# Moving the layer-0 xs stores to ScalarE's transfer queue, and the rank store half a unit later in SyncE's

## The chip, the cores and the metric

One Trainium2 chip, one of its cores. A core has TensorE (PE), VectorE (DVE), ScalarE (ACT), GpSimd (POOL) and SyncE (SP), each with a list of instructions of its own that it works through in order, and 16 DMA engines, which move data between the chip's main memory and the on-chip memory. A transfer is an instruction in the list of some engine: that engine issues it, and goes on while the data moves. Instructions wait for one another by semaphores. The metric is the time of one execution on the device in microseconds (us), less being better.

## The reference

The input x has 4 images of 64 channels and 256x256 points, in float32. Two layers follow one another; only the first is touched by the change.

```python
def layer0(x):                      # called with gn(x), a group norm in 32 groups
    h = gelu(conv3x3(x, c1_w) + c1_b)
    h = c1x1(h, c2_w, c2_b)
    xa, k = split(h, 2, axis=1)
    xs = depthwise_1x3(xa) + sh_b
    xs = depthwise_3x1(xs) + sv_b
    xs = gelu(xs)
    pooled = xs.mean(axis=(2, 3))
    weights = softmax(pooled @ gate_w.T)
    mask = top 2 of the 3 weights, per image, the rest 0
    out = xs
    for i, (w1, b1, w2, b2, w3, b3) in enumerate(experts):   # ranks 2, 4, 8
        e = c1x1(c1x1(k, w2, b2) * c1x1(xs, w1, b1), w3, b3)
        out = out + e * mask[:, i]
    return c1x1(out, proj_w, proj_b)

x = x + layer0(gn(x))
x = x + layer1(gn(x))   # two 3x3 convolutions with 8-bit weights and batch norms over all images
```

What matters for the change: the expert weights of an image depend on the mean of xs over the whole image. So the output of layer 0 can't be formed where xs is made. xs, and the product of the two low-rank maps, are kept in main memory until the image's gate is known, and are read back then.

## The kernel before, in words

*Units.* The front (layer 0) is cut into 64 units: 4 images of NCH = 16 chunks, each of 16 rows of the image. A loop over slots, u = 0 to SLOTS−1 with SLOTS = 67, puts the work of several units side by side: in slot u the convolution of unit u is done, the input for u+1 and u+2 is prepared, the depthwise taps of u−1 and u−2 are finished, and the output of a unit about an image back is formed. The layer's second convolution stage (conv1, conv2 of layer 1) follows it, and the last slots of the front overlap with conv1's first steps.

*Order.* Nothing is left to a scheduler in the main part: all five engines keep the order in which the program's calls are made. That order comes from a table of places. `at_slot(u, pos, call, ...)` puts a call at a place: a pos under 6 is in the first half of slot u, a pos from 6 on in its second half (pos 6.13 comes at order 0.13 there). Calls are then made in the order of their places, and each call appends its instructions to the lists of the engines that it uses. For the slots behind the last unit, a dictionary TAIL (L1023) says at which step of conv1 each call comes.

*Transfers.* All transfers of the loop are issued from SP (`nc.sync.dma_start`). SP's list has, per unit: the load of x (x_load, L508, 1.25 MB, three units ahead); a load of the input of the next image for its statistics (stats_load, L409, 1 MB, tile xs_in); the store of y, layer 0's output (out_store, L861, 1 MB, to y_d); the load of the input into the y tile, to which the layer's result is added (out_load, L803, 1 MB, tile y, of which there are 2); the load of xs back (xs_load, L812, 1 MB); two stores of xs (xs_store, L710, 512 KB each, to xs_d). In every second unit there are two loads of the experts' ranks (low_load, L822, 256 KB each) and one store of the ranks (in front_low, L747, 512 KB, to low_d). Eight completion semaphores are dealt out to the transfers in the order of the program, so a transfer also waits until the one eight before it, which used the same semaphore, has landed.

*Around xs.* Each unit makes two xs tiles, sub 0 and sub 1. For each: front_taps_a and front_taps_b (PE, tile ps_a, one buffer), front_taps_i (ACT, L677: t from ps_a), front_taps_h (DVE, L683, L686, L689: neighbours added in t), front_xs (ACT, L705: xs = gelu(t), its sum kept for the mean), xs_store. An xs tile has 4 buffers. In slot u, sub 1 of unit u−2 has its taps from 2 to 5.2, its gelu at 5.3 and its store at 8.6. Sub 0 of unit u−1 has its taps from 7 on, its gelu in the next slot at 1.55 and its store there at 4.7. Next to them on ACT stand x_four (L526, at 1.58) and the two gelus of front_h (L637, at 6.13 and 6.14).

*Around the ranks.* Over two units, front_k (PE) and front_k_out (ACT, L733, in even slots, at 9.2) form k·w2 in the tile k (1 buffer); front_q (PE, at 8 in odd slots) forms xs·w1; front_low (at 8.1 in odd slots) multiplies them on DVE (L746) and stores the result.

*Around y.* out_open (PE, tile ps_o) projects xs and the ranks with the gate's weights in them, out_add (DVE, L848) adds this to the y tile, out_stats (DVE, L853) takes the statistics of y, and out_store sends it to y_d. The table has out_store at 8.25, between the store of the ranks (8.1) and that of xs sub 1 (8.6).

Of the kernel before, what the change touches and what calls it, by code (L numbers as in the profile page):

```python
# [28 lines left out]
NOCT = NG // 2  # L29
# [12 lines left out]
def conv_preact_kernel(ctx: ExitStack, tc: tile.TileContext, io, col128, colset, col64):  # L42
    nc = tc.nc
# [18 lines left out]
    xs_d = [dram.tile([P, NOCT, 2 * GF], F32, name=f"xs_d{b}") for b in range(B)]  # L62
    low_d = [dram.tile([P, NOCT // 4, 2 * GF], F32, name=f"low_d{b}") for b in range(B)]
# [4 lines left out]
    def flat(t):  # L68
        return t.rearrange("p a b -> p (a b)")
# [50 lines left out]
    def at(step, order, call, *args):  # L120
        plan[step, order].append((call, args))
# [9 lines left out]
    def c128(name):  # L131
        return m128[:, col128[name][0] : col128[name][1]]
# [103 lines left out]
    def weights1_scale():  # L236
        tops = work.tile([P, P, 2], F32, tag="k", name="tops", bufs=1)
        rows = bass.AP(top_d.tensor, top_d.offset, [[0, P], [1, 2 * P]])
        nc.sync.dma_start(tops.rearrange("p a b -> p (a b)"), rows)
        yield  # L240
        for i, name in enumerate(("w1", "w2")):
            nc.vector.tensor_reduce(w_scale[name], tops[:, :, i], AX.X, ALU.max)

    def weights1(name):

        scale = w_scale[name]
        w = mset[0][:, colset[name][0] : colset[name][1]]
        nc.vector.tensor_scalar(scale, scale, 1.0 / QMAX, None, ALU.mult)
        inv = stat.tile([P, 1], F32, tag="s3", name=f"inv_{name}")
        nc.vector.reciprocal(inv, scale)  # L250
        yield
        nc.vector.tensor_scalar(w, w, inv, ROUND, ALU.mult, ALU.add)
        nc.vector.tensor_scalar(w, w, ROUND, None, ALU.subtract)
        nc.vector.tensor_scalar(w, w, QMAX, -QMAX, ALU.min, ALU.max)
        yield
        g = w.rearrange("p (k o) -> p k o", k=3)
        first, second = g[:, :, 0:P], g[:, :, P : 2 * P]
        nc.vector.tensor_copy(wq[name][:, 0], first)
        nc.vector.tensor_tensor(wq[name][:, 1], first, second, ALU.add)
        nc.vector.tensor_scalar(wq[name][:, 2], second, -1.0, None, ALU.mult)  # L260
# [216 lines left out]
    xt, x4s, e2s, mcs, d2s, hs, xss, k_sb, pooled, open_a, open_t = ({} for _ in range(11))  # L477
# [229 lines left out]
    def xs_store(u, sub):  # L707
        b, k = divmod(u, NCH)
        n = 2 * k + sub
        nc.sync.dma_start(xs_d[b][:, n, :], flat(xss[b, n]))  # L710

    def front_k(b, j):

# [29 lines left out]
    def front_low(b, j):  # L743
        ps = ps_q.pop((b, j))
        low = flat(k_sb.pop((b, j)))
        nc.vector.scalar_tensor_tensor(low, ps.rearrange("p s f -> p (s f)"), c128("e_b1"), low, ALU.add, ALU.mult)  # L746
        nc.sync.dma_start(low_d[b][:, j, :], low)  # L747

    ps_q, xs_in, open_o = {}, {}, {}
    wm, out_bias, ys, lows, st_y = {}, {}, {}, {}, {}  # L750
# [263 lines left out]
    def at_each(places, chain):  # L1014

        for place in places:
            at(*place, next, chain, None)
# [3 lines left out]
    SLOTS = UNITS + 3  # L1021

    TAIL = {  # L1023
        (0, 1.15): (0, 1.15), (0, 1.55): (0, 1.55), (0, 4.7): (0, 4.7), (0, 2): (0, 2), (0, 2.2): (0, 2.2),
        (0, 4): (0, 13.2), (0, 4.15): (0, 13.3), (0, 5.2): (0, 13.4), (0, 5.3): (0, 13.5), (0, 8.6): (1, 13.9),
        (0, 9.2): (3, 13.35), (0, 7): (2, 13.2), (0, 7.2): (2, 13.25), (0, 8): (3, 13.1), (0, 9): (3, 13.2), (0, 9.1): (3, 13.3),
        (1, 1.15): (3, 13.4), (1, 1.55): (3, 13.5), (1, 4.7): (4, 13.9), (1, 2): (5, 13.2), (1, 2.2): (5, 13.25),
        (1, 4): (6, 13.2), (1, 4.15): (6, 13.3), (1, 5.2): (6, 13.4), (1, 5.3): (6, 13.5), (1, 8.6): (7, 13.9),
        (1, 8): (8, 13.2), (1, 8.1): (8, 13.3),
    }  # L1030

    def at_slot(u, pos, call, *args):

        step, order = (2 * u, pos) if pos < 6 else (2 * u + 1, pos - 6)
        if u >= UNITS:
            step, order = TAIL[u - UNITS, pos]
            step += CONV1
        at(step, order, call, *args)

    def plan_front():  # L1040
        last = UNITS - 1
        at_slot(0, 0, x_load, 2)
        at_slot(0, 1.25, next, first_end, None)
        at_slot(0, 1.36, next, first_end, None)
        for u in range(SLOTS):
            if u + 3 <= last:
                at_slot(u, 0, x_load, u + 3)
            if u <= last:
                at_slot(u, 1, front_conv, u, (1, 2))
                at_slot(u, 1.1, front_copy, u, 0)  # L1050
                at_slot(u, 1.3, front_conv, u, (3, 4))
                at_slot(u, 1.35, butterfly_a, u)
                at_slot(u, 1.4, front_copy, u, 1)
                at_slot(u, 2.1, butterfly_b, u)
                at_slot(u, 4.05, butterfly_c, u)
                at_slot(u, 6.12, butterfly_d, u)
                at_slot(u, 6.13, front_h, u, True)
                at_slot(u, 5, front_conv, u, (0, 5))
                at_slot(u, 6.14, front_h, u, False)
            if u + 1 <= last:  # L1060
                if u == 0:
                    at_slot(u, 0.5, x_differences, 1)
                at_slot(u, 1.2, x_scaled, u + 1)
                at_slot(u, 1.31, v_inner, u + 1, 0)
                at_slot(u, 2.3, v_inner, u + 1, 1)
                at_slot(u, 5.5, v_outer, u + 1)
            if u + 2 <= last:
                at_slot(u, 1.58, x_four, u + 2)
                at_slot(u, 2.4, x_fourths, u + 2)
                at_slot(u, 6.6, x_seconds, u + 2, (0, 2))  # L1070
                at_slot(u, 7.3, x_seconds, u + 2, (4, 6))
            if 0 <= u - 2 <= last:
                at_slot(u, 2, front_taps_a, u - 2, 1)
                at_slot(u, 2.2, divide)
                at_slot(u, 4, front_taps_b, u - 2, 1)
                at_slot(u, 4.15, front_taps_i, u - 2, 1)
                at_slot(u, 5.2, front_taps_h, u - 2, 1)
                at_slot(u, 5.3, front_xs, u - 2, 1)
                at_slot(u, 8.6, xs_store, u - 2, 1)
            if 0 <= u - 1 <= last:  # L1080
                at_slot(u, 7, front_taps_a, u - 1, 0)
                at_slot(u, 7.2, divide)
                at_slot(u, 9, front_taps_b, u - 1, 0)
                at_slot(u, 9.1, front_taps_i, u - 1, 0)
                at_slot(u + 1, 1.15, front_taps_h, u - 1, 0)
                at_slot(u + 1, 1.55, front_xs, u - 1, 0)
                at_slot(u + 1, 4.7, xs_store, u - 1, 0)
            j = (u - 2) // 2
            if u % 2 == 0 and 0 <= j < UNITS // 2:
                at_slot(u, 8, front_k, *divmod(j, NOCT // 4))  # L1090
                at_slot(u, 9.2, front_k_out, *divmod(j, NOCT // 4))
            if u % 2 and 0 <= j < UNITS // 2:
                at_slot(u, 8, front_q, *divmod(j, NOCT // 4))
                at_slot(u, 8.1, front_low, *divmod(j, NOCT // 4))
        for b in range(B):
            t = NCH * (b + 1)
            if b < B - 1:
                places = (t + 1, 8.3), (t + 2, 1.25), (t + 2, 1.36), (t + 2, 1.52), (t + 2, 6.15), (t + 2, 8.3), (t + 2, 9.06)
                chain = gate(b)
                for place in places:  # L1100
                    at_slot(*place, next, chain, None)
            else:
                at_each(((CONV1 + 12 + n, 12.7) for n in (1, 3, 3, 4, 8, 12, 16)), gate(b))

        at_slot(1, 1.6, weights1_load)
        at_slot(3, 6.2, weights1_top)
        chain = weights1_scale()
        at_slot(4, 1.45, next, chain, None)
        at_slot(4, 6.2, next, chain, None)
        for i, name in enumerate(("w1", "w2")):  # L1110
            chain = weights1(name)
            for n in range(3):
                at_slot(7 + 3 * i + n, 6.2, next, chain, None)
# [67 lines left out]
    def plan_conv1(b):  # L1181
# [31 lines left out]
        at(t + NG + 3, 13.3, conv1_close, b)  # L1213

    plan_front()
    for b in range(B):
        if b < B - 1:
# [125 lines left out]
    with tc.manual_schedule(  # L1343
# [8 lines left out]
        n = len(chunks)  # L1352
# [62 lines left out]
    for i, (b, k) in enumerate(steps):  # L1415
# [9 lines left out]
        j = i - 3 + KEEP  # L1425
# [113 lines left out]
```

## Time and profile before

| | us |
|---|---|
| runs before | 3035.65, 3042.23, 3040.98 (median 3040.98) |
| the profiled execution | 3027.39 |
| its span in the trace | 3025.4 |
| front, units of layer 0 (changed) | about 0 to 1350 |
| conv1 and conv2 of layer 1 | about 1360 to 2600 |
| last stage, sums and output | about 2600 to 3025 |
| issue of one xs store on SP: least, median, most | 0.319, 0.383, 2.752 |

The page has the share of each engine over the whole span, then 40 slices of 75.6 us: a digit is a tenth of the slice in which the engine was busy, for DMA the mean over the 16 DMA engines. A list of waits gives, for an instruction's line, what it waited for, with the sum in us, the number of times and the longest one. SPq is the queue of SP, which has only transfers to issue. A row of windows gives, from left to right, the length of the stretch, the busy time of PE, PE's weight loads (PEld), DVE, ACT and POOL with their counts, PE's clock, the share of the transfers' time and what was moved in GB/s. A row of the timeline has start, duration, engine, line, operation and output <- input; a bracket at its end tells how long the engine idled before it, and what ended that. In all of these a wait for several things is put down to the one that came last.

The last 425 us are bound by transfers (425 GB/s, in the page's last slices), and the two convolution stages by PE in their larger part. None of them holds an instruction of the change, except for the last few xs stores and the last rank store, which TAIL puts into conv1's first steps.

### The profile page before, as it was taken

How to read it: one execution, taken by the hardware profiler on the slowest of the kernel's cores; microseconds unless marked ns; L12 is line 12 of the kernel's file. 1: busy time of each engine (PE TensorE's matmuls, PEld its weight loads, DVE VectorE, ACT ScalarE, POOL GpSimd, SP SyncE). 2: the span in 40 equal slices, each digit the busy share in tenths (PEclk: the TensorE clock that was granted, in tenths of full speed). 3: DMA queues.
4: the chain of work that ended last, by engine and by line, in shares of the span. 5: the costliest groups of instructions: out<-in, count | busy, mean ns of one | idle time of the engine just before them, and what ended most of it. 6: DMA issues, size and time to landing. Idle time of an engine off the chain costs nothing.

```text
span 3025.4 us, 53036 instructions
## 1 busy us (share of the span) xinstructions
PE 2364.3 (78%) x21576; PEld 1504.4 (50%) x21576; DVE 2467.0 (82%) x2793; ACT 2054.0 (68%) x2274; POOL 1677.4 (55%) x1210
## 2 busy tenths in 40 slices
PE   1898899998999999978889999989999999100000
PEld 1444444444544445545556667767888888100000
DVE  5668688888888899968788888979998998876665
ACT  6798887786876555556566677878888888432222
POOL 5888887776877778834445455635555555000000
PEclk9999999999999999999999999999999999655555
DMA  8565479999999879849889898756777763899999
GB/s 344 188 238 224 185 263 371 350 349 346 342 341 329 301 280 328 291 157 322 315 327 332 336 339 321 262 207 238 257 273 262 266 243 138 333 425 424 424 425 410
DMA packets 135572, 915.35 MB, mean 303 GB/s; under 512 B 14944, under 2 KB 15712, under 8 KB 40608
## 3 DMA queue, kind: packets, MB, share of 16 engines
q1 hardware_dynamic: 135328, 911.97, 80.3%
q8 instruction: 169, 2.77, 0.4%
q14 instruction: 75, 0.61, 0.1%
HBM read 573.74 MB, written 338.17 MB: 301 GB/s over the span
## 4 chain that ended last, share of the span: by engine, by line
PE 28%; DMA 18%; DVE 5%; issue 2%; ACT 1%; SPq 1%; POOL 0%; DVEq 0%; ACTq 0%
PE ps_h L295 18%; PE ps_h2m L295 6%; DMA y_end<-y_d 5%; DMA h<-h_d 4%; DMA out<-h 4%; PE ps_hm L295 3%; DMA y<-in_xp 3%; DMA xs_in<-xs_d 2%; PE ps_o L492 2%; DVE h L317 1%; DVE diff L352 1%; DVE y L848 1%; DVE odd L361 1%; DMA y_d<-y 1%; SPq L822 0%
## 5 line engine op out<-in xcount | busy, mean ns | idle before, releaser
L295 PE MATMUL ps_h<-diff,w_q 128*128 128x512 f32 x3072 | 751.3, 399 | 9.1 <-DVE h L317 9.1
L295 PEld LDWEIGHTS ps_h<-diff,w_q 128*128 128x128 f32 x3072 | 577.1, 189 | 180.9 <-issue 25.8
L492 PE MATMUL ps_c<-v,us 64*64 64x256 f32 x9216 | 547.2, 386 | 41.4 <-DVE ps_c L623 35.6
L342 POOL TENSOR_TENSOR d<-yn 128x1024 f32<-128x1024 f32 x128 | 355.0, 2793 | 313.7 <-DMA yn<-y_d 179.8
L492 PEld LDWEIGHTS ps_c<-v,us 64*64 64x64 f32 x9216 | 363.6, 136 | 199.8 <-DVE ps_c L623 44.9
L342 POOL TENSOR_TENSOR d<-h 128x1024 f32<-128x1024 f32 x127 | 311.9, 2477 | 194.8 <-DVE diff L350 130.0
L492 PE MATMUL ps_a<-h,av 64*64 64x512 f32 x4080 | 387.9, 493 | 38.8 <-DVE t L686 28.7
L317 DVE SCALAR_TENSOR_TENSOR h<-ps_h,scale_w,m 128x1024 f32<-128x1024 f32 x256 | 323.6, 1279 | 64.2 <-PE ps_h L295 48.1
L540 POOL TENSOR_TENSOR x<-x 128x512 f32<-128x512 f32 x256 | 330.3, 1290 | 12.5
L1420 ACT ACTIVATE v<-y_end,shift,gn 128x2048 f32<-128x2048 f32 x64 | 133.8, 2093 | 279.7 <-DMA y_end<-y_d 244.5
L492 PEld LDWEIGHTS ps_a<-h,av 64*64 64x64 f32 x4080 | 153.9, 134 | 307.5 <-issue 204.3
L381 ACT ACTIVATE junk<-h,less_h 128x2048 bf16<-128x2048 f32 (+3 forms) x133 | 255.9, 1924 | 11.1 <-DVE h L317 10.9
L848 DVE SCALAR_TENSOR_TENSOR y<-ps_o,ob,y 128x1024 f32<-128x1024 f32 x128 | 163.9, 1280 | 118.9 <-DMA y<-in_xp 62.9
L1421 DVE SCALAR_TENSOR_TENSOR h<-h,ss,v 128x2048 f32<-128x2048 f32 x64 | 149.8, 2350 | 120.8 <-ACT v L1420 80.3
L683 DVE SCALAR_TENSOR_TENSOR t<-ps_a,m,t 128x1020 f32<-128x1020 f32 x128 | 163.3, 1276 | 104.1 <-ACT t L677 102.7
L677 ACT ACTIVATE t<-ps_a,tap_bias,m 128x1024 f32<-128x1024 f32 x128 | 154.1, 1204 | 97.8 <-PE ps_a L492 97.3
L705 ACT ACTIVATE xs<-t 128x1024 f32<-128x1024 f32 x128 | 134.9, 1054 | 121.2 <-DVE t L689 92.6
L295 PE MATMUL ps_h2m<-odd,w_q 128*128 128x512 f32 x768 | 193.2, 400 | 8.2 <-DVE odd L361 4.4
L295 PE MATMUL ps_hm<-odd,w_q 128*128 128x512 f32 x768 | 193.0, 400 | 4.2 <-ACT k L733 2.4
L352 DVE SCALAR_TENSOR_TENSOR diff<-d,gn,diff 128x1024 fp32r<-128x1024 f32 x128 | 188.1, 1499 | 4.7 <-ACT diff L345 4.7
L345 ACT ACTIVATE diff<-d 128x1024 fp32r<-128x1024 f32 x128 | 135.1, 1055 | 83.4 <-POOL d L342 82.1
L532 POOL TENSOR_TENSOR x<-x,x 128x512 f32<-128x512 f32 x128 | 161.0, 1279 | 43.3 <-ACT x L526 43.3
(226 smaller groups left out, 4321.8 us busy)
## 6 DMA issues: line engine op xcount, KB each, us to landing
h_d<-h SPq DMA_DIRECT2D x114, 1024.0 KB
x<-in_xc SPq DMA_DIRECT2D x64, 1280.0 KB
h<-h_d SPq DMA_DIRECT2D x64, 1152.0 KB
yn<-y_d SPq DMA_DIRECT2D x60, 1152.0 KB
xs_in<-in_xp SPq DMA_DIRECT2D x64, 1024.0 KB
xs_d<-xs SPq DMA_DIRECT2D x128, 512.0 KB
xs_in<-xs_d SPq DMA_DIRECT2D x64, 1024.0 KB
y<-in_xp SPq DMA_DIRECT2D x64, 1024.0 KB
```

The costliest lines, as they stand in the source:

```text
L295: nc.tensor.matmul(ps, wq[w][:, kind, kx, :], t[:, rows, kx : kx + W], start=(j == 0), stop=(j == len(terms) - 1))
L317: nc.vector.scalar_tensor_tensor(h.rearrange("p (e k) w -> p e (k w)", e=2), ps.rearrange("p e k w -> p e (k w)"), w_scale[w], m.unsqueeze ...
L342: engine.tensor_tensor(raw.rearrange("p (g r) w -> p g r w", g=2), *pair, ALU.subtract)
L352: nc.vector.scalar_tensor_tensor(lower, raw, scale, upper.bitcast(F32), ALU.mult, ALU.subtract)
L381: nc.scalar.activation(junk[rows, 0:n], flat(h), AF.Square, bias=less[name][rows], accum_out=total)
L492: last[:] = [nc.tensor.matmul(ps[o, at_out[0] : at_out[1], :], w[i], rhs[i], **flags)]
L532: nc.gpsimd.tensor_tensor(x4[:, j - 1], x_rows(u, j + 2), x4[:, j - 1], ALU.subtract)
L540: nc.gpsimd.tensor_tensor(x[:, r : r + 2], x[:, r + 2 : r + 4], x[:, r : r + 2], ALU.subtract)
L677: nc.scalar.activation(flat(t), flat(ps), AF.Identity, bias=tap_bias, scale=sh[:, 1:2])
L683: nc.vector.scalar_tensor_tensor(t[:, :, 1:W], ps[:, :, 0 : W - 1], sh[:, 0:1], t[:, :, 1:W], ALU.mult, ALU.add)
L848: nc.vector.scalar_tensor_tensor(y, ps.rearrange("p x s w -> p x (s w)"), out_bias[b], y, ALU.add, ALU.add)
L1421: nc.vector.scalar_tensor_tensor(h, h, ss2[:, 0:1], v, ALU.mult, ALU.add)
```

## The change

xs_store issues its transfer from ScalarE's list (`nc.scalar.dma_start`) instead of SP's, and comes earlier in the slot: for sub 0 at 1.6 in place of 4.7, for sub 1 at 6.135 in place of 8.6. On ACT that is right behind x_four, and between the two gelus of front_h. Both stand one ACTIVATE behind the gelu that made the tile.

front_low no longer stores the ranks. The new function low_store does, again from SP's list, at 11.9 of the odd slot, which is its end and just before the next slot's x_load; before, the store was made at 8.1. So out_store at 8.25 now comes ahead of it.

TAIL has the new places for the same steps of conv1, except for the last store of ranks, which comes at step 9, order 13.9 (before with front_low, at step 8, order 13.3).

In counts: SP issues 846 transfers (974 before) and ACT 128 (none before). The instructions of PE, DVE and POOL are the same, in the same order; ACT's other instructions too.

```diff
     def xs_store(u, sub):
         b, k = divmod(u, NCH)
         n = 2 * k + sub
-        nc.sync.dma_start(xs_d[b][:, n, :], flat(xss[b, n]))
+        nc.scalar.dma_start(xs_d[b][:, n, :], flat(xss[b, n]))
...
         nc.vector.scalar_tensor_tensor(low, ps.rearrange("p s f -> p (s f)"), c128("e_b1"), low, ALU.add, ALU.mult)
-        nc.sync.dma_start(low_d[b][:, j, :], low)
+        low_of[b, j] = low
+
+    low_of = {}
+
+    def low_store(b, j):
+        nc.sync.dma_start(low_d[b][:, j, :], low_of.pop((b, j)))
...
     TAIL = {
-        (0, 1.15): (0, 1.15), (0, 1.55): (0, 1.55), (0, 4.7): (0, 4.7), (0, 2): (0, 2), (0, 2.2): (0, 2.2),
-        (0, 4): (0, 13.2), (0, 4.15): (0, 13.3), (0, 5.2): (0, 13.4), (0, 5.3): (0, 13.5), (0, 8.6): (1, 13.9),
+        (0, 1.15): (0, 1.15), (0, 1.55): (0, 1.55), (0, 1.6): (0, 1.6), (0, 2): (0, 2), (0, 2.2): (0, 2.2),
+        (0, 4): (0, 13.2), (0, 4.15): (0, 13.3), (0, 5.2): (0, 13.4), (0, 5.3): (0, 13.5), (0, 6.135): (1, 13.9),
...
-        (1, 8): (8, 13.2), (1, 8.1): (8, 13.3),
+        (1, 8): (8, 13.2), (1, 8.1): (8, 13.3), (1, 11.9): (9, 13.9),
     }
...
-                at_slot(u, 8.6, xs_store, u - 2, 1)
+                at_slot(u, 6.135, xs_store, u - 2, 1)
...
-                at_slot(u + 1, 4.7, xs_store, u - 1, 0)
+                at_slot(u + 1, 1.6, xs_store, u - 1, 0)
...
                 at_slot(u, 8, front_q, *divmod(j, NOCT // 4))
                 at_slot(u, 8.1, front_low, *divmod(j, NOCT // 4))
+                at_slot(u, 11.9, low_store, *divmod(j, NOCT // 4))
```

## The prediction

> **What bounds the kernel now.** I read the slices first, then the chain of waits, then the windows, the waits of SP's queue, the waits of the engines, and last two stretches of the timeline.
>
> ```profile
> PE 2364.3 (78%) x21576; PEld 1504.4 (50%) x21576; DVE 2467.0 (82%) x2793; ACT 2054.0 (68%) x2274; POOL 1677.4 (55%) x1210
> ...
> DMA  8565479999999879849889898756777763899999
> ```
>
> Over the whole span no engine is full. The chain that ended last begins only at 1358 us, behind the part that changes, so the change must be priced in the front (0 to 1350 us), and there by stretches:
>
> ```profile
> core 0: us, PE busy (x) PEld busy (x) DVE busy (x) ACT busy (x) POOL busy (x), PEclk, DMA share, GB/s
> 100.00:400.00 300.00, 266.33 (x3802) 141.15 (x3800) 220.42 (x277) 267.74 (x390) 252.30 (x232) 0.97 0.58 210
> 400.00:1000.00 600.00, 565.30 (x7847) 292.00 (x7842) 517.17 (x686) 453.05 (x628) 461.63 (x424) 0.99 0.93 340
> 1110.00:1250.00 140.00, 139.58 (x1972) 71.86 (x1968) 127.43 (x156) 80.18 (x101) 115.10 (x106) 1.00 0.92 328
> ```
>
> From 100 to 400 us PE and ACT are both near 89% and the transfers at 58%. From 400 to 1000, PE is at 94% and the transfers at 93%: two near-bounds, and PE idles 35 us in all. From 1110 to 1250 PE is full. So 35 us is the ceiling on what transfers could give back in the long middle, and nothing is to be had from 1110 to 1250. From 480 to 740 two units take 40.4 to 40.7 us, against 37.1 from 1110 to 1250.
>
> What SP's queue waits for, in the whole program:
>
> ```profile
> SPq L803 <- DMA y_d<-y: 272.6, 41, 15.6
> SPq L747 <- DVE k L746: 213.9, 30, 11.9
> SPq L861 <- DVE y L848: 193.3, 42, 9.1
> SPq L710 <- ACT xs L705: 177.6, 33, 11.7
> ```
>
> The second and the fourth are what the change takes out of SP's way: 391 us of a queue standing at a store whose data isn't ready. But in the window 480 to 1000 they are only 70.1 and 4.3 us, and SP's waiting matters only where an engine waits for a transfer. There, the waits of the engines say:
>
> ```profile
> ACT t L677 <- PE ps_a L492: 48.0, 27, 2.8
> ...
> DVE y L848 <- DMA y<-in_xp: 23.1, 7, 4.2
> ```
>
> PE's own waits there for what the transfers bring are 8.0 us for DVE's y and 3.9 us for xs_in, 11.9 us together. From 100 to 400 us no engine waits for a transfer of this loop, though SP stands at the xs store for 104.0 us between 100 and 480.
>
> **What the Trainium skill says.** "DMA: Bandwidth & Descriptors", section "Issuing engines are not separate DMA queues": transfers of ScalarE and SyncE run on the same 16 DMA engines and interleave, and several issuers save only the time of issuing. The trace agrees as far as it can: from 480 us on, 1 MB lands every 2.44 to 2.5 us, so more issuers can't make bytes faster. The same page, "Queues, rings and completion order": each queue row has rings of its own, a DMA engine goes round between rings by packets, and within a ring descriptors start in order. The trace of before has one ring for all loop transfers (q1), in which 18 to 20 us pass from issue to landing at the peak; how two rings share shows in no run yet.
>
> **The change part by part.** The sum is made against the profiled execution, 3027.39 us (span 3025.4), which lies 13.6 us below the median of 3040.98.
>
> *Bytes.* None are added or removed: per two units the same 13.5 MB (two each of x 1.25, y, xs_in, stats and y_d 1 MB, four xs and a rank store of 0.5, two rank loads of 0.25). The DMA floor of the middle stretch stays.
>
> *Issue on ACT.* 128 stores, 0.383 us each (median of the xs_d row on SP, 0.319 to 2.75), would be 49 us with no cover. Each is queued right after an ACTIVATE that has just begun: x_four (L526) for sub 0, the first gelu of front_h (L637) for sub 1, both 1.05 us long, while the gelu that made xs has ended. So the issue lies beside them. If the cover fails, only 100 to 400 us pays, where ACT is near a bound: 34 stores by 0 to 0.38 us, 0 to 13 us. In this trace an ACTIVATE starts 0.1 us before the one ahead has ended; an instruction between may break this overlap. I take 0.1 us each: +3 us. A gain from it is excluded, as ACT gets nothing off its list.
>
> *Waits on ACT.* Eight completion semaphores are dealt to the transfers in program order, so every transfer also waits until the one eight before it has landed. On SP this was a wait of the transfer queue; on ACT the t (L677), gelus and xs behind it wait too. Held against the landings of before, the sub 1 stores wait for something that landed 0.3 to 5 us earlier, and in units 0 to 17 everything has landed by 6 us or more. The sub 0 stores of even slots 22 to 44 wait for a store y_d. Slot 28: that y_d, issued at 596.04, landed at 607.44, while the next instruction on ACT, t L677, began at 605.15:
>
> ```profile
> 601.67 1.05 ACT L526 ACTIVATE x<-x 128x1024 f32<-128x1024 f32 x1
> ...
> 605.15 1.21 ACT L677 ACTIVATE t<-ps_a,tap_bias,m 128x1024 f32<-128x1024 f32 x1 [2.43 <-PE ps_a L492]
> ...
> 606.39 1.28 DVE L683 SCALAR_TENSOR_TENSOR t<-ps_a,m,t 128x1020 f32<-128x1020 f32 x1 [0.47 <-ACT t L677]
> ```
>
> Behind t come L683 and L686 on DVE, and PE's next ps_a began at 609.13, right after L686: a late t is a late PE. Nine such slots, with 2.3, 4.1, 4.0, 2.7, 3.7, 2.0, 3.5, 4.6 and 0.9 us, make 28 us if the y_d stores land as before.
>
> *The rank store moved.* But they don't. In odd slots low_d stood ahead of y_d on SP:
>
> ```profile
> 590.10 1.27 DVE L848 SCALAR_TENSOR_TENSOR y<-ps_o,ob,y 128x1024 f32<-128x1024 f32 x1
> ...
> 594.35 1.28 DVE L746 SCALAR_TENSOR_TENSOR k<-ps_q,m,k 128x1024 f32<-128x1024 f32 x1 [0.46 <-PE ps_q L741]
> ```
>
> ```profile
> 595.66 0.33 SPq L747 DMA_DIRECT2D low_d<-k  x1
> 596.04 0.43 SPq L861 DMA_DIRECT2D y_d<-y  x1
> ```
>
> Its y was there at 591.37, 4.67 us before the issue. It now goes first: sooner by up to 4.7 us at the issue, and at the landing by at least the 1.23 us that 512 KB ahead of it took; I take 2.5, since the queue is short there. Then the nine stalls shrink to 0, 1.6, 1.5, 0.2, 1.2, 0, 1.0, 2.1 and 0: 7.6 us. Half of it falls into time in which PE would have waited for y later: +4 us. The rank store itself waits a half unit longer; its readers are an image away, but there is one k tile, and the next k (L733 on ACT) must wait for its landing. In slot 28 x, before which it now stands, was issued at 597.35; behind y_d it lands near 608.7 (607.44 plus its 1.23), and L733 began at 616.25. Cost 0, hidden by a margin of 7.5 us; a landing 18 to 20 us after the issue, as at the peak, would use that up and stop ACT for a microsecond or so.
>
> *The transfers' gain.* y loads follow the landing of the y_d two before, so 2.5 us sooner in every second unit, against a mean lateness of 23.1/7 = 3.3 us. I take all of PE's 11.9 us as gone, with the late xs_in among them: −12 us (0 to −35 from both sides). The load of x, behind an xs store and the rank store in SP's queue, is now behind the rank store alone. Around the change of image and from 1250 to 1350 us the yn loads stood 0.4 us behind an xs store (1286.83 and 1287.25): −2 us. After 1360 the order of transfers is the same: 0.
>
> Sum: +3 +4 −12 −2 = −7 us, 3020 in the profiled execution, 3034 on the median.
>
> **The rivals.**
> 1. *Small gain (my forecast)*, 3034, its own range 3018 to 3035 (−6 to −23). For: SP no longer stands before stores, and y was late. Against: the gain depends on PE's last 6%.
> 2. *The stalls on ACT win (slower).* The store's wait for the transfer eight back holds t L677, at slots 22 to 44. Price: the full 28 us if y_d lands as late as before, since xs stores from the second ring cut in between its packets; −12 −2 +3 +28 = +17, 3058. It decides from the point at which the remaining stalls pass about 17 us, that is if y_d lands less than some 1.2 us sooner. For: DVE and PE follow t without a gap. Against: the rank store has left from before it.
> 3. *Nothing to be measured*, within 0.2% (6 us, which is about what a measurement of this kernel can tell from no change), 3041: the middle is bound by bytes (93% share), so gains and stalls both vanish in the transfers' slack.
> 4. *The two rings share badly or well*: stores that nobody waits for take turns with loads that are waited for, or they fill gaps in which SP stood still. Shares of 0.93 leave at most 35 us of gain; 1% of 600 us of loss is 6.
>
> **How the numbers follow.** Forecast with the good half of rival 4: 0.44; rival 3: 0.20; rival 2 with the other half: 0.36. The range takes 3008 (about the middle of the ceiling of 35 and twice the sum) to 3062 (rival 2 with issue costs of 4 us more). Both signs hold much of the chance, so the forecast's own range stands above.
>
> **What would show it.** Right: the y_d store of odd slots directly after DVE's y; the waits of SP at the xs store gone; y waits for its load less than 23.1 us from 480 to 1000; ACT's t idle for transfers under 10 us; two units at about 40 us. Wrong: t L677 waiting for a y_d or x transfer for 20 us or more, or PE busy in fewer of the 300 us from 100 to 400, with ACT idle between gelus. Wrong altogether would be a change in the stretch after 1360 us, which I hold to be untouched.

## The result: 0.3 to 0.4% less, and the profile after

| | us, median (lowest to highest) | runs | ratio to before, 95% interval |
|---|---|---|---|
| before | 3039.82 (3033.64 to 3042.23) | 6 | |
| after | 3025.00 (3018.93 to 3030.36) | 6 | 0.9958 (0.9943 to 0.9973) |
| after again (a2), beside the experiments | 3028.45 (3018.32 to 3036.93) | 22 | 0.9971 (0.9961 to 0.9981) |

The change makes the kernel faster by 0.3 to 0.4%, some 9 to 13 us. The forecast was 3034, 7 us under the median of then. The profiled execution of after took 3030.36 us, the slowest of its six, and that of before 3027.39, less than any of the six above; so the two spans (3028.6 and 3025.4) stand the wrong way round, and only stretches of them are compared here. The front shows the gain: measured at the start of the last unit (its first copy L605 on ScalarE), it had taken 1295.9 us before, and 1285.8 and 1284.6 in two profiles of after. Behind the front, every later profile of a kernel with the rank loads as they were took 4 to 24 us longer than that one profile of before, whatever it changed.

The queues of transfers, from the page of after (queue, packets, MB, share of the 16 engines' span):

```profile
q1 hardware_dynamic: 116896, 844.85, 74.7%
q10 hardware_dynamic: 18432, 67.12, 5.6%
```

The 128 stores are a ring of their own now; before, q1 had all 911.97 MB. Their row among the operations on the tile xs_d (ns least/median/most):

```profile
L710 ACTq DMA_DIRECT2D xs_d<-xs x128: 326/326/353, 107.4 to 1343.3; - x128
```

On SP an issue of the same transfer took up to 2752 ns, on ScalarE never over 353.

The waits of SP's list in after, whole program:

```profile
SPq L866 <- DVE y L853: 418.0, 64, 16.2
...
SPq L808 <- DMA y_d<-y: 233.7, 35, 15.8
SPq L752 <- DVE k L746: 177.4, 30, 24.9
```

L866, L808 and L752 are out_store, out_load and low_store. The wait for xs (177.6 us) is gone, and SP stands 418 us at the y_d store in place of 193.3: it comes there earlier, and stands before the data it is meant to send next. The rank store's wait (177.4 us, 213.9 before) is still in SP's list too. SP's waits have not become fewer; they are at another place.

The same stretches as shown of before (length, busy time of PE, PEld, DVE, ACT and POOL, clock, share of the transfers, GB/s), first of after:

```profile
100.00:400.00 300.00, 266.23 (x3843) 139.68 (x3835) 222.22 (x284) 269.91 (x394) 253.57 (x234) 0.98 0.60 216
```

PE did as much as before (266.33) from 100 to 400. Where the gain lies shows best between units, as the stretches shift in time. From the start of unit 20 to that of unit 34 it took 281.1 us before, and 273.8 and 275.7 after; from 34 to 50, 320.8 before, 317.6 and 317.8 after; from 50 to 63, 255.9 before, 255.2 and 255.8 after. So 5 to 7 of the 10 to 11 us come from units 20 to 34, the stretch with most transfers in it. Here is that stretch in the same window of 280 us, before:

```profile
440.00:720.00 280.00, 263.77 (x3668) 136.16 (x3664) 238.66 (x306) 215.91 (x305) 215.82 (x199) 1.00 0.95 352
```

and after:

```profile
440.00:720.00 280.00, 269.26 (x3772) 137.35 (x3768) 246.16 (x316) 219.79 (x310) 219.22 (x203) 1.00 0.95 362
```

The transfers are busy for the same share, 0.95, and yet moved 362 GB/s in place of 352. This line holds the question of the study: the prediction had said that the bytes set a floor, and a floor of bytes doesn't give way by 3%.

PE's own waits for what the transfers bring, from 480 to 1000 us, before:

```profile
PE ps_o L492 <- DVE y L848: 8.0, 7, 1.3
...
PE ps_o L492 <- DMA xs_in<-xs_d: 3.9, 6, 0.9
```

and after, where the second is gone:

```profile
PE ps_o L492 <- DVE y L853: 7.2, 5, 1.7
```

At slot 28 the step that the prediction worked out is seen in the timeline of after (start, duration, engine, line, operation):

```profile
585.78 1.27 DVE L853 SCALAR_TENSOR_TENSOR y<-ps_o,ob,y 128x1024 f32<-128x1024 f32 x1
590.10 1.28 DVE L746 SCALAR_TENSOR_TENSOR k<-ps_q,m,k 128x1024 f32<-128x1024 f32 x1 [0.53 <-PE ps_q L741]
```

```profile
587.08 0.33 SPq L866 DMA_DIRECT2D y_d<-y  x1
591.41 0.33 SPq L752 DMA_DIRECT2D low_d<-k  x1
591.84 0.40 SPq L508 DMA_DIRECT2D x<-in_xc  x1
```

y was there at 587.05 and its store left at 587.08; before, 4.67 us lay between. By the landing events it landed at 599.59, 12.5 us behind the y, against 16.1 before. And ScalarE's store of sub 0, eight transfers on, waited for exactly this landing:

```profile
597.41 1.05 ACT L526 ACTIVATE x<-x 128x1024 f32<-128x1024 f32 x1
599.67 0.35 ACTq L710 DMA_DIRECT2D xs_d<-xs  x1
600.83 1.21 ACT L677 ACTIVATE t<-ps_a,tap_bias,m 128x1024 f32<-128x1024 f32 x1 [2.37 <-PE ps_a L492]
```

A hold is here the time from the end of the activation ahead (598.46) to the issue of the store: 1.2 us. Over the whole of after the holds make 8.6 us, in the second profile 8.0. The prediction had 7.6.

### The profile page after: what moved, and what is told of

The parts are those of the page before. It is cut to its first block, busy times and chain, and to the rows that moved or that the text cites. A ratio compares the mean times of both kernels' runs of the same rounds, so it can differ in the third digit from the quotient of the medians.

```text
span 3028.6 us, 52918 instructions
## 1 busy us (share of the span) xinstructions
PE 2359.3 (78%) x21576; PEld 1500.1 (50%) x21576; DVE 2477.7 (82%) x2793; ACT 2052.2 (68%) x2274; POOL 1675.0 (55%) x1210
## 4 chain that ended last, share of the span: by engine, by line
PE 28%; DMA 19%; DVE 6%; issue 2%; ACT 1%; SPq 0%; POOL 0%; DVEq 0%; ACTq 0%
PE ps_h L295 18%; PE ps_h2m L295 6%; DMA y_end<-y_d 5%; DMA out<-h 4%; DMA h<-h_d 4%; DMA y<-in_xp 4%; PE ps_hm L295 3%; DMA xs_in<-xs_d 2%; PE ps_o L492 1%; DVE h L317 1%; DVE diff L352 1%; DVE odd L361 1%; DVE y L853 1%; DMA y_d<-y 1%; DVE h L1428 0%
## 5 line engine op out<-in xcount | busy, mean ns | idle before, releaser
L492 PE MATMUL ps_c<-v,us 64*64 64x256 f32 x9216 | 539.7, 383 | 42.4 <-DVE ps_c L623 36.7
L492 PEld LDWEIGHTS ps_c<-v,us 64*64 64x64 f32 x9216 | 357.0, 135 | 201.3 <-DVE ps_c L623 47.1
L381 ACT ACTIVATE junk<-h,less_h 128x2048 bf16<-128x2048 f32 (+3 forms) x133 | 255.9, 1924 | 11.1 <-DVE h L317 11.0
```

Source lines behind the costliest of these rows:

```text
L381: nc.scalar.activation(junk[rows, 0:n], flat(h), AF.Square, bias=less[name][rows], accum_out=total)
L492: last[:] = [nc.tensor.matmul(ps[o, at_out[0] : at_out[1], :], w[i], rhs[i], **flags)]
```

## The experiments

All times are medians; ratios are to the kernel before, measured on the same chip beside each of them. The edits below leave out the same moves in TAIL.

| kernel | us | ratio, 95% interval | runs |
|---|---|---|---|
| e1: xs stores moved, rank store not | 3048.22 | 1.0032 (1.0019 to 1.0045) | 11 |
| e2: rank store moved, xs stores not | 3028.85 | 0.9977 (0.9967 to 0.9987) | 22 |
| e3: new places, all from SP | 3029.74 | 0.9978 (0.9964 to 0.9992) | 14 |
| e4: ScalarE's list, old places | 3030.68 | 0.9979 (0.9968 to 0.9991) | 17 |
| h3: e1 with sub 0 from SP | 3042.81 | 1.0025 (1.0015 to 1.0036) | 14 |
| h1: after with sub 0 from SP | 3039.11 | 1.0013 (1.0002 to 1.0024) | 22 |
| v42: after, sub 0's store behind t | 3021.79; again 3020.75 | 0.9955 (0.9939 to 0.9970); 0.9940 (0.9927 to 0.9952) | 6; 6 |
| s0: before, straight rank loads | 2970.57 | 0.9774 (0.9760 to 0.9789) | 5 |
| s1: after, straight rank loads | 2972.08 | 0.9777 (0.9765 to 0.9790) | 4 |
| s2: e1, straight rank loads | 2966.52 | 0.9764 (0.9750 to 0.9777) | 4 |

### One part alone, the place alone, the list alone

e1 is after with the rank store back at its old place:

```diff
-                at_slot(u, 11.9, low_store, *divmod(j, NOCT // 4))
+                at_slot(u, 8.1, low_store, *divmod(j, NOCT // 4))
```

> Only the first part: xs stores from ScalarE's list at the new places; the rank store stays at 8.1 in SP's list, ahead of y_d. Theory A (a free SP queue and the second ring make the gain, the rank store adds little): 3026 to 3030 us against 3040 before, front shorter by 7 to 10 us. Theory B (the rank store's move makes it, as my prediction's sum had it: y_d sooner, and ScalarE's waits small only because of it): 3040 to 3058, with t L677 waiting for a y_d store by 10 to 28 us in the stretch 480 to 1000.

e2 is after with the xs stores as before:

```diff
-        nc.scalar.dma_start(xs_d[b][:, n, :], flat(xss[b, n]))
+        nc.sync.dma_start(xs_d[b][:, n, :], flat(xss[b, n]))
...
-                at_slot(u, 6.135, xs_store, u - 2, 1)
+                at_slot(u, 8.6, xs_store, u - 2, 1)
...
-                at_slot(u + 1, 1.6, xs_store, u - 1, 0)
+                at_slot(u + 1, 4.7, xs_store, u - 1, 0)
```

> Only the second part: the rank store at 11.9, all xs stores in SP's list at their old places. Theory A: 3036 to 3040 (little or nothing). Theory B: 3026 to 3032, because y_d of odd slots goes sooner by up to 4.7 us.

e3 is after with only the first of these three edits; e4 is after with only the other two.

> All the new places of the change, but the xs stores issued from SP's list, so one ring. Theory A: 3038 or more, since at place 1.6 SP stands before the gelu of xs with the y load behind it. Theory C (not the ring and not SP's queue, but the places, make the gain): 3025 to 3030, as the change.

> The xs stores in ScalarE's list, but at the old places 4.7 and 8.6; the rank store at 11.9. Theory A (what counts is that they are out of SP's list): 3024 to 3030, as the change. If the place on ScalarE counts, because the issue there needs cover or the xs tile is freed later: 3032 to 3045, seen as idle time of ScalarE around the stores.

Theory A fell with e1: the xs stores alone make the kernel slower, by 0.3%. The rank store alone makes it faster, by 0.2%, as theory B had it, and the two parts don't add up: +10 us and −7 us apart, −9 to −13 together. Whether the whole change is faster than the rank store's move alone isn't settled, as the intervals overlap (0.9967 to 0.9987 for e2, 0.9943 to 0.9973 and 0.9961 to 0.9981 for the change). e3 gives what e2 gives, so the earlier places on SP bring nothing more, and theory C is out, though its number came true; e4 too gives no more than e2.

In e1 the holds of ScalarE are large, as the losing case of the prediction had them. The longest, in the timeline of e1:

```profile
500.66 1.05 ACT L526 ACTIVATE x<-x 128x1024 f32<-128x1024 f32 x1
506.44 0.33 ACTq L710 DMA_DIRECT2D xs_d<-xs  x1
506.81 1.20 ACT L677 ACTIVATE t<-ps_a,tap_bias,m 128x1024 f32<-128x1024 f32 x1 [5.11 <-PE ps_a L492]
```

The bracket puts the idle 5.11 us before t down to PE's ps_a, but the store stands between, held for 4.7 us. What it waited for is a load of the statistics' input, issued at 482.13 behind the rank loads and landed at 506.4, 24 us later; it is the transfer eight before in the order of e1. Nine such holds make nearly all of 31.5 us in the trace. Units 20 to 34 took 293.1 us, 12 more than before. It looks like the whole answer. But DVE's list has y ahead of its work on t, and in DVE's timeline of the same kernel y comes later still:

```profile
508.92 1.28 DVE L853 SCALAR_TENSOR_TENSOR y<-ps_o,ob,y 128x1024 f32<-128x1024 f32 x1 [6.30 <-DMA y<-in_xp]
```

DVE waited 6.30 us for the y load, until 508.92, and t had ended at 508.01. Without the hold, t would have lain there. It is the same in eight of the nine: DVE waits 3.8 to 6.3 us for its y load and comes to t 0.7 to 2.1 us after t has ended. (In the ninth, of 0.5 us, DVE waits for t.) So the holds of e1, large as they are, cost DVE next to nothing. What was late in e1 is the y loads.

### Holds taken away

h3 is e1, and h1 is after, with sub 0 back in SP's list, so that no store on ScalarE is held (the traces show 0.0 and 0.3 us of holds):

```diff
-        nc.scalar.dma_start(xs_d[b][:, n, :], flat(xss[b, n]))
+        (nc.scalar if sub else nc.sync).dma_start(xs_d[b][:, n, :], flat(xss[b, n]))
...
-                at_slot(u + 1, 1.6, xs_store, u - 1, 0)
+                at_slot(u + 1, 4.7, xs_store, u - 1, 0)
```

> As e1 (rank store at 8.1), but only the sub 1 stores are in ScalarE's list; sub 0 is back in SP's at 4.7. Theory A (e1 lost because its sub 0 stores held ScalarE, 31 us in nine places from 460 to 930 us): the holds go, 3028 to 3040, front within 5 us of before's. Theory B (e1 lost because two rings share badly, with stores cutting in ahead of loads): still slower than before, by 4 us or more.

> As the change, but with sub 0 back in SP's list at 4.7. Theory A (the remaining holds of 8.5 us cost, and SP's list gains little from being rid of sub 0): 3022 to 3027, as the change or up to 4 us better. Theory B (each store out of SP's list brings its share): between e2 and the change, 3027 to 3031.

v42 keeps sub 0 in ScalarE's list but moves it behind t:

```diff
-                at_slot(u + 1, 1.6, xs_store, u - 1, 0)
+                at_slot(u + 1, 4.2, xs_store, u - 1, 0)
```

> As the change, but sub 0's store stands on ScalarE at 4.2, behind t (L677) and ahead of the statistics' activations, so that a hold no longer keeps t from DVE and PE. Theory A (holds of t cost what they last): up to 8 us better than the change, 3017 to 3025. If the holds are in slack: as the change. If the earlier place at 1.6 is itself worth something, since the xs tile and the transfers come earlier: 3026 to 3032.

a2 is after once more:

> The changed kernel unchanged, run beside the others: ratio to before 0.994 to 0.998 (first measured 0.9958). Its profile tells how much of the 13 us by which the first profile of the change was longer than that of before behind 1360 us is chance, and whether the 4.6 us it lost between slots 18 and 20 come back: by chance, they go; if they belong to the change, they stay.

h3 has no holds and is still slower than before by 0.25%, as its theory B forecast: units 20 to 34 took 290.1 us, against 293.1 in e1. That fits what e1's trace says of the holds. It can't price them, for its edit does more than take holds away: in h1 the same edit, with only 8 us of holds to lose, made after slower by some 10 us. h1 was a miss for both theories: half of the stores on each list is slower than all on SP (e2) and than all on ScalarE. The price of a hold is better read from v42, where one place alone moves: the holds fall from 8 to 2.7 to 3.0 us, and the stretch from 273.8 and 275.7 to 272.5 and 272.3, so 1 to 3 us for 5. In after itself DVE idled 1.7 us before t at the held places, and 2.6 in a2. In a2 the stretch of units 18 to 20 took 39.9 us as everywhere, against 44.6 in the first profile of after; that loss was chance.

What goes with the time, roughly, in all of these is a wait of SP that I had passed over. It stands in front of the x load (L508) and the xs load (L812, after the edits L817), whose semaphore is that of a rank load eight before. In before, from 440 to 720 us:

```profile
SPq L508 <- DMA ranks<-low_d: 23.7, 7, 4.7
...
SPq L812 <- DMA ranks<-low_d: 17.8, 7, 4.6
```

after:

```profile
SPq L817 <- DMA ranks<-low_d: 17.2, 7, 3.2
...
SPq L508 <- DMA ranks<-low_d: 15.0, 6, 3.3
```

and in h3, without a single hold:

```profile
SPq L508 <- DMA ranks<-low_d: 34.4, 7, 6.0
...
SPq L817 <- DMA ranks<-low_d: 25.2, 7, 4.8
```

The sum of the two waits, from 440 to 720 us, beside the time from unit 20 to unit 34, for every profile of a kernel with the rank loads as they were:

| | wait for rank loads, us | units 20 to 34, us |
|---|---|---|
| v42 (two profiles) | 31.7, 28.1 | 272.5, 272.3 |
| after (two profiles) | 32.2, 32.4 | 273.8, 275.7 |
| e2 | 30.1 | 277.5 |
| e3 | 31.9 | 277.5 |
| e4 | 39.1 | 279.7 |
| before | 41.5 | 281.1 |
| h1 | 50.2 | 282.3 |
| h3 | 59.6 | 290.1 |
| e1 | 59.3 | 293.1 |

It isn't a strict order: e2 and e3 wait less than after and are slower. And that two things go together doesn't tell which is cause. The last three runs take the slow loads out.

### The rank loads on all DMA engines

A rank load takes four groups of 16 rows out of low_d. In the trace its semaphore is counted up by five separate events, that of every other transfer of the loop by sixteen. This agrees with the Trainium skill, "DMA: Bandwidth & Descriptors", section "Why a DMA increments its semaphore by 16 and not by 1": a transfer is spread over the largest number of engines, up to 16, that divides the slowest dimension of both sides (here 4), and the engines that aren't used are counted at once. By the landing events of before, from unit 20 to 34, a rank load of 256 KB lands 3.5 us behind the transfer ahead of it, while 1 MB of statistics' input takes 2.5. The edit, which puts the rows in the wrong order, so that the output is no longer right:

```diff
-            low = low_d[b][:, k // 2, :].rearrange("(i x r) f -> x i r f", i=4, x=2)
+            low = low_d[b][:, k // 2, :].rearrange("(x p) f -> x p f", x=2)
```

> The kernel before, with one edit: each load of ranks takes 64 consecutive rows of low_d, not four groups of 16. Same bytes, same number of transfers, the same places; the rows come in the wrong order, so the ranks' part of layer 0's output is computed from other rows. Theory R (the two rank loads, which only four DMA engines carry, are what the middle stretch waits for): units 20 to 34 fall from 281 us to 262 to 270, the whole to 3010 to 3022. Theory Q (SP's list and ScalarE's holds are): units 20 to 34 stay at 276 or more.

> The changed kernel with the same edit of the rank loads (ranks' rows in the wrong order). Theory R: units 20 to 34 within 3 us of s0, the ratio of this to before no more than 0.2% under that of s0, so that the change brings next to nothing once the four-engine loads are gone. Theory Q: it stays 7 us or more under s0 there, as it is without the edit.

> e1 with the same edit of the rank loads (ranks' rows in the wrong order). Theory R: the 12 us that e1 lost from unit 20 to 34 go, within 4 us of s0; ScalarE's holds fall to under 8 us, as what held it were loads queued behind the ranks. Theory Q: it stays 8 us or more over s0.

The loads then have sixteen events, and in s0 land 1.1 us behind the one ahead. What the loads on four engines did to the rest shows in the landing events of all other transfers: from unit 20 to 34, the last of the sixteen came 7.8 us behind the twelfth in before, in the mean, and 1.2 us in s0. So four engines were behind with everything. A y store and the y load that waits for it, in before:

```profile
489.12 0.33 SPq L861 DMA_DIRECT2D y_d<-y  x1
...
509.10 0.33 SPq L803 DMA_DIRECT2D y<-in_xp  x1
```

Twelve of the store's landing events had come by 500.25, the last four came from 507.64 to 509.02. SP issued nothing from 500.40 to 509.10, and by the records of DMA packets mostly four or five were in flight from 508.4 to 510.1. The same comes back every 40 us or so, up to 710. Over the window 440 to 720, exactly four were in flight for 10.3 us in before and 1.1 in s0.

Before, after and e1 with this edit take the same: 0.9774, 0.9777, 0.9764, with intervals that overlap. Units 20 to 34 take 266.4, 265.8 and 265.8 us, as theory R forecast. For the whole of s0 it was wrong: 2970.57 us, where 3010 to 3022 was forecast. A gain of that size is what the front alone brings, 22 us up to the last unit; but 20 of the 64 rank loads come later, beside conv1, and from the last unit to the last rank load (at 1800.4 us before, 1748.4 in s0) another 30 us go. The wait of SP for a rank load is not in the list of any of the three, ScalarE's holds are 0.1 us in s1 and s2, and the window of s1 reads:

```profile
440.00:720.00 280.00, 273.04 (x3836) 140.45 (x3836) 251.59 (x324) 225.73 (x319) 226.00 (x209) 0.99 0.96 372
```

PE is at 273.04 of 280, the transfers at 372 GB/s with nearly the same share. And SP's list in s1, in that window:

```profile
SPq L866 <- DVE y L853: 156.7, 15, 14.3
SPq L808 <- DMA y_d<-y: 41.2, 7, 7.4
SPq L752 <- DVE k L746: 24.8, 7, 3.6
```

SP stands at the y_d store for more than half of the window, and no cost of it can be seen. So theory R holds in the middle stretch: what the change gains, and what e1 loses, is there only with the slow rank loads. They leave four DMA engines behind, and the other twelve run out of work while SP waits for a store that the four still hold. With that gone, it makes no measurable difference which list the xs stores are in.

Some things stay open. With the rank loads spread, PE is busy for nearly the whole window, so that there is little left to gain and room for a late transfer to be hidden in; the three runs show that the slow loads are needed for gain and loss, not each step from the order of SP's list to the time. And the lag of the four engines doesn't put the other kernels in order (6.2 us both in after, second in the table of waits, and in e1, its last). Nor does idle time of DMA engines explain the 362 GB/s in place of 352, since the share stayed. What changed is the time of packets: one of 8 KB took 309 ns in the median in all of these kernels, but 357 in the mean before, 345 in after, 376 in e1 and 328 in s0. Why some packets take so long isn't shown.

## Why the prediction was right, and where by luck

Right in its main line: faster, by 9 to 13 us where 7 was forecast. Step by step:

- *y_d sooner.* Held. It left 0.03 us behind its y at slot 28 in place of 4.67, and landed 3.5 us sooner counted from the y, where I took 2.5. e2 shows that this part alone brings 0.23%.
- *Holds of ScalarE.* The mechanism and its size held: 8.6 and 8.0 us against 7.6, at the sub 0 stores, mostly on y_d. The price of half a microsecond for each, +4, may have been too high: DVE idled 1.7 and 2.6 us for t at these places, and v42 gives 0.2 to 0.6 of a microsecond for each. It isn't settled closer than that.
- *Rival 2*, in which the holds win and the whole is slower, was right about e1's size (31.5 us against 28) for a wrong reason: in e1 the eighth transfer back is not y_d but an input load behind the rank loads, since moving the rank store also moves it in the count. And its price was wrong: at eight of the nine holds DVE was waiting for y longer than for t.
- *Rival 4*, two rings that share well or badly, isn't settled: with two rings e1 and h3 lost, while after, s1 and s2 did not, so two rings alone don't decide it.
- *Issue on ScalarE*, taken at +3: not seen. PE and ACT from 100 to 400 did what they did before (266.23 and 269.91 us), and units 0 to 12 took 212.6 and 215.7 us against 217.6.
- *The transfers' gain*, taken at −12: all of PE's 11.9 us of waits from 480 to 1000 were to go, and 7.2 us of them were left (7.7 in a2), all for y; so 4 to 5 us came by this way, and the waits of PE don't say where the rest of the front's 10 to 11 us came from. y itself waited 15.1 us for its load (11.0 in a2) in place of 23.1. What I had not seen is in the term that I had put at nothing: "None are added or removed ... The DMA floor of the middle stretch stays." The bytes stayed and the floor didn't: a share of 0.93 to 0.95 is a mean over 16 engines, of which four were behind, and it counts the time of packets, not what they carry. s0 moves the same bytes and takes 15 us less from unit 20 to 34.
- *SP's waits.* The 391 us that were to be taken out of SP's way had the rank store's 213.9 in them. That store stayed in SP's list, and SP stood 177.4 us at it; only the xs stores' 177.6 went.
- *−2 around the change of image and the yn loads*: 0.1 to 0.7 us from unit 50 to 63, so next to nothing there.
- *Nothing behind the front*: not settled, as the profiles differ there by more than the change is worth.
- *The range.* Its low end, 3008, isn't the middle of 35 and twice 7, which would be some 3016; nothing hung on it.

That the total came out is partly luck: one cost not there (+3), one price perhaps too high (+4), one gain less than half of what it was put at (−12), one not seen (−2), and the slow rank loads, without which there is nothing to gain, overlooked.

## A version that is probably better

v42, one place in the table moved, was 0.9955 and 0.9940 of before in two measurements. In the second its interval (0.9927 to 0.9952) lies under that of the change's larger measurement (0.9961 to 0.9981); in the first (0.9939 to 0.9970) the two overlap. It keeps the change and lets t go ahead of the store. The 68 us of s0 are a measure of what the rank loads cost, not a version: a kernel in which they go over all engines with the rows in the right order wasn't tried.

## What to carry to other kernels

A high mean share of the transfers needn't be a bound by bytes: look for transfers that are slow for their size, and for what is issued only when they have landed. When a change of queues helps or hurts, take the slow transfer out of both versions before you believe a story about queues. And a wait that is seen in the trace, like the holds here, has a price only if nothing else was late at that moment.

## What the runs showed of the hardware

- Two rings at once: transfers from ScalarE's ring went in between those of SP's. From unit 20 to 34, an xs store landed 8.8 us after its issue in after, against 16.4 us in before's one ring and 16.0 in e3, which has the places of after on one ring, with the bytes the same. So the second ring changed more than the time of issuing.
- The issue of the same 512 KB store took 0.383 us in the median and up to 2.75 on SP's list, and 0.326 to 0.353 on ScalarE's.
- A load on four DMA engines left these behind for the transfers that followed: 7.8 us from the twelfth to the sixteenth landing event in before, 1.2 in s0.
- Moving one transfer changes what every later one waits for, as the completion semaphores are dealt by count over both lists: e1 and after differ in the place of one store, and the held sub 0 stores wait for an input load in the one, mostly for y_d in the other.
- Why half of the stores on each list (h1) is slower than all on either isn't explained. Its wait for the rank loads (50.2 us) goes with it, and why it rose isn't known.
